# Graph network kernel: the second transposing pass of layer 1 written earlier, and layer 2's blocks written among layer 1's last blocks

## The chip, the cores and the metric

The kernel runs on one core of one Trainium2 chip. The metric is device time in microseconds (us). The kernel before took 1979.47 us, the median of 3 runs (1973.92 to 1994.36).

## What is computed

Four graph layers run over 2708 nodes with 128 features each. Every layer adds its result to `x` and normalises the row.

```python
x = _layernorm(x + _L0_gnn_ref(x, adj))   # msg = adj.T @ x, divided by the column sums of adj
x = _layernorm(x + _L1_gnn_ref(x, adj, ...))
x = _layernorm(x + _L2_gnn_ref(x, adj, ...))
x = _layernorm(x + _L3_gnn_ref(x, adj, ...))

# layer 1: messages over the edges, then an update of each row
messages = gelu(s[:, None, :] + d[None, :, :] + msg_b)      # s, d = x @ the two halves of msg_w
aggregated = einsum('ijd,ij->id', messages, adj)
h = gelu(concat(x, aggregated) @ upd_w.T + upd_b) + x       # then a layer norm

# layer 2: one dense product with adj, then a batch norm over the nodes
h = adj @ (x @ W) + b
h = gamma * (h - mean(h, 0)) * rsqrt(var(h, 0) + EPS) + beta
```

`adj` is 2708 x 2708 in float32 and has about 16 entries other than zero in a row. Layer 3 is an attention over the same edges.

## The kernel before

**Stages.** The rows of `adj` are cut into 22 blocks, 21 of 128 rows and one of 20 (`BLOCKS`). Layer 0 loads them one by one into a ring of nine buffers (`load`, L392 to L396, pool `ring`), multiplies each on TensorE (L411), and searches the entries of each row with VectorE (`extract`, L420 to L475). The 13 blocks of the first group (`SPLIT` = 13) are searched in layer 0. The other nine still stand in the ring when layer 1 starts, and are searched there. Each row's list of neighbours goes into a table in DRAM, sorted by the number of neighbours inside the two groups; `perm` holds which node stands at which place.

**Layer 1** goes over 22 blocks of sorted nodes. `own_row(b)` (L791) gathers the block's own rows. `messages(b)` (L797 to L827) gathers one neighbour at a time for all 128 rows with an indirect DMA on POOL's queue (`gather`, L236, issued at L237), `CAPS[b]` of them: 32, 24, 21, ... for the first group, and 31, 22, 20, 18, 17, 16, 14, 13, 10 for blocks 13 to 21. They are handled in chunks of up to eight, each chunk in one of five buffers `msg`. TensorE turns the own rows (L802) and multiplies them (L804), VectorE adds that product to the chunk (L813), ScalarE takes the Gelu (L816), and VectorE sums the neighbours up with their weights (L822, L824). The PSUM tile `own` has one buffer, so one block's messages are worked on at a time. `update(b)` (L829 to L865) multiplies the sums, normalises twice, writes the new rows `x_n` (L311) to DRAM by an indirect DMA of POOL's queue (`scatter`, issued at L245), turns `x_n` on TensorE (L860) and multiplies it by layer 2's weight (L864) into `xw[b]` (L865).

**The transposed matrix.** Layer 2 needs, for each block of sorted nodes, the matching columns of `adj`. `transposed(e, rows)` (L867 to L889) turns block `e` on TensorE (L877, 22 transposes), copies them on ScalarE (`at_sb`, three buffers, L882), and writes them to `at_dram` with seven DMAs of SP's queue (L884). The nine blocks of the second group are turned while they stand in the ring. The 13 of the first group are loaded a second time. In the program that is written after the updates of blocks 9 to 12, four, four, four and one at a time.

**Layer 2** is a loop of its own that is written behind layer 1. For each block `b` it gathers 128 rows of `at_dram` (L926, issued at L237; 1.39 MB), and adds 22 products into six PSUM banks `accs2` (L929; each float32 matmul is two instructions, so 44 for a block). A row of `at_dram` is whole only when all 22 blocks have been turned, so no block of layer 2 can be gathered before that. Behind it lie the batch norm (L985 to L1062) and layer 3.

**What sets the order.** Only VectorE in layer 0, and three engines in layer 3, follow the order of the program (`manual_schedule`). In layers 1 and 2 a planner lays out each engine's queue from the whole program; each queue is then worked through strictly in turn. The planner moves instructions a long way. In the kernel before, TensorE's queue holds all 484 transposes ahead of block 0 of layer 2, and that block stands ahead of the update of block 9, though the program writes layer 2 behind all of layer 1.

Below, A(e) stands for layer 2's block `e` (its gather, or its 44 TensorE instructions), and x2(b) for the writing of `x_n` of block `b`.

Of the kernel before, what the change touches and what calls it, by code (L numbers as in the profile page):

```python
# [9 lines left out]
FP = mybir.dt.float32  # L10
# [5 lines left out]
P = 128  # L16
N = 2708
D = 128
NFULL = N // P
NREM = N - NFULL * P  # L20
NBLK = NFULL + 1
# [19 lines left out]
SPLIT = 13  # L41
# [19 lines left out]
BLOCKS = [(b * P, min(P, N - b * P)) for b in range(NBLK)]  # L61


ORDER = [*range(20), 21, 20]
# [15 lines left out]
def gnn_resnorm_kernel(  # L80
# [21 lines left out]
    nc = tc.nc  # L102
# [103 lines left out]
    at_dram = tables.tile([NBLK * P, N], FP, name="at_dram")  # L206
# [7 lines left out]
    perm = keep.tile([P, NBLK], I32, name="perm")  # L214
# [21 lines left out]
    def gather(dst, table, index):  # L236
        nc.gpsimd.indirect_dma_start(  # L237
            out=dst,
            out_offset=None,
            in_=table[0:N, :],  # L240
            in_offset=bass.IndirectOffsetOnAxis(ap=index, axis=0),
        )
# [82 lines left out]
    def banks(name):  # L325
        return [bank.tile([P, 512], FP, name=f"{name}{i}", tag="bank") for i in range(6)]

    with ExitStack() as layer:
        ring = layer.enter_context(tc.tile_pool(name="ring", bufs=RING))
# [62 lines left out]
        def load(b):  # L392
            r0, n = BLOCKS[b]
            rows = ring.tile([P, N], FP, name="rows", tag="rows")
            nc.sync.dma_start(rows[0:n, :], adj[r0 : r0 + n, :])
            return rows  # L396
# [110 lines left out]
        def ranked(g):  # L507
            b0, b1 = GROUPS[g]
            rows = min(N, b1 * P) - b0 * P
            nc.vector.tensor_scalar(  # L510
                rank[:, b0:b1], above[g], 0.5, 0.5 * (rows - 1) + b0 * P, ALU.mult, ALU.add
            )
# [43 lines left out]
        def sorted_lists(g):  # L556
            b0, b1 = GROUPS[g]
            full = min(b1, NFULL)
            parts = [(b0, full, P)] + ([(NFULL, NBLK, NREM)] if b1 > full else [])
            for c0, c1, n in parts:  # L560
                nc.sync.dma_start(
                    ls[0:n, c0:c1, :],
                    lists_dram[c0 * P : c0 * P + (c1 - c0 - 1) * P + n, :].rearrange(
                        "(b p) w -> p b w", p=n
                    ),
                )
                nc.vector.tensor_copy(idx[0:n, c0:c1, :], ls[0:n, c0:c1, SLOTS : 2 * SLOTS])
                nc.vector.tensor_copy(perm[0:n, c0:c1], ls[0:n, c0:c1, 2 * SLOTS + 1])
                nc.vector.tensor_tensor(
                    wrong[0:n, c0:c1, 3], ls[0:n, c0:c1, 2 * SLOTS], caps[0:n, c0:c1], ALU.is_gt  # L570
                )

        def load3(b):

            k, j = BLOCKS3[b]
            mine_3 = lists3[:, b % 6, :]
            for r in range(4):
                r0 = BASE3[b] + r * j * k
                nc.sync.dma_start(
                    mine_3[32 * r : 32 * r + j * k, :], lists_dram[r0 : r0 + j * k, :]  # L580
                )
            n, r0 = 4 * j * k, BASE3[b]
            nc.sync.dma_start(
                node3[0:n, b, :], lists_dram[r0 : r0 + n, 2 * SLOTS : LW]
            )

        def beside3(b):

            if b < SPLIT + 2:
                return list(range(FIRST3))[2 * max(b - 3, 0) : 2 * max(b - 2, 0)]  # L590
            return list(range(FIRST3, NB3))[2 * (b - SPLIT - 2) : 2 * (b - SPLIT - 1)]
# [66 lines left out]
        def run(steps):  # L658
            for _ in steps:
                pass  # L660
# [31 lines left out]
        for jb in (20, 21):  # L692
            m, at = BLOCKS[jb][1], (jb - 20) * (D + 1) + D
# [95 lines left out]
        xw = xs  # L789

        def own_row(b):  # L791
            n = BLOCKS[b][1]
            x_s = mine.tile([P, D], FP, name="x_s", bufs=3)
            gather(x_s[0:n, :], x1_dram, perm[0:n, b : b + 1])
            return x_s

        def messages(b, x_s, three):  # L797
            n, kk = BLOCKS[b][1], CAPS[b]
            po = own_ps.tile([P, 512], FP, name="own", tag="own")
            x_st, s_ps = mine.tile([P, P], FP, name="x_st"), po[:, P : 2 * P]  # L800
            acc = (po[:, 0:P], po[:, 3 * P : 4 * P])
            nc.tensor.transpose(po[:, 0:n], x_s[0:n, :], ident[0:n, 0:n])  # L802
            nc.scalar.copy(x_st[:, 0:n], po[:, 0:n])
            nc.tensor.matmul(s_ps[0:n], lhsT=x_st[:, 0:n], rhs=ws_t, start=True, stop=True)  # L804
            parts = mine.tile([P, 2, D], FP, name="parts")
            cuts = chunks_of(kk)
            for c0, c1 in cuts:
                kc = c1 - c0
                msg = msgs.tile([P, 8, D], FP, name="msg")
                for k in range(kc):  # L810
                    gather(msg[0:n, k, :], d_dram, idx[0:n, b, c0 + k : c0 + k + 1])
                mk = msg[0:n, 0:kc, :]
                nc.vector.tensor_tensor(  # L813
                    mk, mk, s_ps[0:n].unsqueeze(1).to_broadcast((n, kc, D)), ALU.add
                )
                nc.scalar.activation(mk, mk, AF.Gelu)  # L816
                for k in range(c0, c1):
                    last, m = acc[k % 2][0:n], msg[0:n, k - c0, :]
                    to = parts[0:n, k % 2, :] if k >= kk - 2 else last
                    v = ls[0:n, b, k : k + 1]  # L820
                    if k < 2:
                        nc.vector.tensor_scalar(to, m, v, None, ALU.mult)  # L822
                    else:
                        nc.vector.scalar_tensor_tensor(to, m, v, last, ALU.mult, ALU.add)  # L824
            for i, b3 in enumerate(three):
                spread(b3, po, 256 + 64 * i)
            return x_st, parts  # L827
# [39 lines left out]
        def transposed(b, rows):  # L867

            r0, n = BLOCKS[b]
            for j0 in range(0, NBLK, 4):  # L870
# [9 lines left out]
                for a, e, m in ((0, full, P), (full, count, NREM)):  # L880
                    if e > a:
# [6 lines left out]
                            at[0:m, a:e, 0:n],  # L888
                        )  # L889

        ahead = own_row(0)
        waiting = None
        left = list(range(SPLIT, NBLK))
        for b in range(NBLK):
            if b == SPLIT - 2:
                sorted_lists(1)
            x_s, ahead = ahead, own_row(b + 1) if b + 1 < NBLK else None
            three = beside3(b)
            if b == 2 or b == SPLIT + 1:
                for b3 in beside3(b + 1):  # L900
                    load3(b3)
            for b3 in beside3(b + 2) if three or beside3(b + 1) else []:
                load3(b3)
            x_st, agg = messages(b, x_s, three)
            for _ in range(2 if b < 1 else 1):
                if left:
                    e = left.pop(0)
                    run(extract(e, rows_of[e]))
                    transposed(e, rows_of[e])
                    if e == SPLIT:  # L910
                        ranked(1)
                    if e == NBLK - 3:
                        run(place(SPLIT, NBLK - 2, lists(SPLIT, NBLK - 2)))
                    if e == NBLK - 1:
                        run(place(NBLK - 2, NBLK, lists(NBLK - 2, NBLK)))
            update(b, x_s, x_st, agg)
            if not left and b >= 9:
                for e in range(4 * (b - 9), min(SPLIT, 4 * (b - 8))):
                    transposed(e, load(e))


        accs2 = banks("acc2_")
        for b in range(NBLK):
            n = BLOCKS[b][1]
            at = ring.tile([P, N], FP, name="at_rows", tag="rows")
            gather(at[0:n, :], at_dram, perm[0:n, b : b + 1])  # L926
            for ib in range(NBLK) if b == 0 else ORDER:
                i0, m = BLOCKS[ib]
                nc.tensor.matmul(  # L929
                    accs2[ib // 4][0:m, (ib % 4) * D : (ib % 4 + 1) * D],  # L930
                    lhsT=at[0:n, i0 : i0 + m],
                    rhs=xw[0:n, b, :],
                    start=(b == 0 and ib % 4 == 0),
                    stop=(b == NBLK - 1 and ib in (3, 7, 11, 15, 19, 20)),
                )

# [19 lines left out]
    with ExitStack() as layer:  # L958
# [28 lines left out]
        for b0, count, n in quads():  # L987
            a = accs2[b0 // 4].rearrange("p (j d) -> p j d", d=D)[0:n, b0 % 4 : b0 % 4 + count]
            nc.vector.tensor_tensor(hb[0:n, b0 : b0 + count], a, broad(b_row, n, count), ALU.add)
            for b in range(b0, b0 + count):  # L990
                nc.tensor.matmul(
                    ps_m[:, 0:D], lhsT=ones[0:n, :], rhs=hb[0:n, b, :],
                    start=(b == 0), stop=(b == NBLK - 1),
# [4 lines left out]
        for b0, count, n in quads():  # L998
# [4 lines left out]
            for j in range(count):  # L1003
                nc.tensor.matmul(
                    ps_v[:, 0:D], lhsT=ones[0:n, :], rhs=sq[0:n, j, :],
                    start=(b0 + j == 0), stop=(b0 + j == NBLK - 1),
# [6 lines left out]
        for b0, count, n in quads():  # L1013
# [34 lines left out]
            for j in range(count):  # L1048
                at = slice(j * P, j * P + n)
# [17 lines left out]
    with ExitStack() as layer:  # L1067
# [341 lines left out]
        for i, (b, j) in enumerate(quads):  # L1409
            g, jj = BLOCKS3[b]  # L1410
            e = g * (P // g)
# [550 lines left out]
```

## Time and profile before

| what | value |
|---|---|
| median of 3 runs | 1979.47 us |
| the profiled execution, its own time | 1674.75 us |
| its span | 1673.0 us |
| layer 0 | up to about 224 us |
| first gather of layer 1 | 223.9 us |
| first gather of block 13's messages | 587.6 us |
| first and last gather of `at_rows` | 548.4 and 856.7 us |
| last TensorE instruction of L929 | 881.0 us, running |
| batch norm | 881 to 960 us |
| layer 3 | 960 to 1673 us |

The profiled execution is 304.7 us shorter than the median of the runs. No view shows why; sums below are made against the profiled execution.

The profile's groups give, for one line and one engine, busy time and the mean duration of one instruction, and behind the second bar the idle time just before and what ended most of it. The waits add up who waited for whom. The timeline gives the instructions of one engine in order of time: start, duration, line, and in brackets the idle time before. Windows give busy time by engine for a stretch. PE is TensorE, PEld its weight loads, DVE VectorE, ACT ScalarE, POOL GpSimd, and SPq the queue of SP.

### The profile page before, as it was taken

The numbers are of one execution on the slowest core, as the hardware profiler recorded it, in microseconds if no ns is written. First come the engines' busy times: TensorE is split into PE (matmuls) and PEld (weight loads), VectorE is DVE, ScalarE is ACT, GpSimd is POOL, SyncE is SP. The second block draws the span as 40 slices with busy tenths as digits, with TensorE's granted clock in tenths as the row PEclk, the third lists the DMA queues.
The fourth block names the chain that finished last, engine by engine and source line by source line (L and its number), as shares of the span: only waits on it lengthen the run. The fifth ranks groups of instructions, "written<-read, shape, count | busy, mean of one in ns | idle before, by whom it ended". The sixth has DMA issues, their size and how long they took to land. (4 is left out here: it accounts for less than half of the span.)

```text
span 1673.0 us, 24020 instructions
## 1 busy us (share of the span) xinstructions
PE 1197.2 (72%) x5876; PEld 850.9 (51%) x5876; DVE 1215.7 (73%) x5697; ACT 695.7 (42%) x2635; POOL 916.7 (55%) x1007
## 2 busy tenths in 40 slices
PE   5996654455626544463795769988989988998994
PEld 5996543334414533463684325554555555555553
DVE  9999966777747571455444479788889888898883
ACT  4959543433314120111111534454545545554552
POOL 0000247777775677777610578665656666666530
PEclk9997555555555666686796856776677777767675
DMA  9433277798937524342531687976666766867630
GB/s 352 179 128 123 50 213 170 206 230 239 258 90 181 168 60 117 119 148 84 190 138 45 201 273 206 233 215 190 192 191 203 214 190 166 231 190 221 190 92 8
DMA packets 162245, 288.49 MB, mean 172 GB/s; under 512 B 44342, under 2 KB 115890, under 8 KB 155015
## 3 DMA queue, kind: packets, MB, share of 16 engines
q0 software_dynamic: 61120, 191.23, 40.8%
q1 hardware_dynamic: 95893, 90.69, 17.5%
q10 hardware_dynamic: 5082, 4.94, 1.0%
q8 instruction: 49, 0.80, 0.2%
q14 instruction: 101, 0.83, 0.2%
HBM read 242.74 MB, written 43.97 MB: 171 GB/s over the span
## 5 line engine op out<-in xcount | busy, mean ns | idle before, releaser
L237 POOL DMA_INDIRECT g<-t_dram,idx x400 | 402.3, 1006 | 195.1 <-issue 133.4
L237 POOL DMA_INDIRECT msg<-d_dram,idx x398 | 376.9, 947 | 124.6 <-issue 103.6
L1254 ACT ACTIVATE sum_junk<-g 126x128 bf16<-126x128 f32 (+3 forms) x800 | 235.3, 296 | 117.0 <-DVE g L1246 66.1
L929 PE MATMUL acc<-x_nat,at_rows 128*128 128x128 f32 (+2 forms) x968 | 155.5, 318 | 119.9 <-DMA at_rows<-at_dram,perm 119.9
L1223 PE MATMUL z<-x,copies 32*126 32x512 f32 (+3 forms) x800 | 212.3, 887 | 30.4 <-DVE g L1423 29.7
L877 PE MATMUL pt_a<-ident,rows 128*128 128x128 f32 (+1 forms) x484 | 115.6, 393 | 145.8 <-ACT at_sb L882 145.6
L929 PEld LDWEIGHTS acc<-x_nat,at_rows 128*128 128x128 f32 (+2 forms) x968 | 140.0, 225 | 130.7 <-DMA at_rows<-at_dram,perm 110.8
L1423 DVE TENSOR_TENSOR g<-g,z 126x1536 f32<-126x1536 f32 (+3 forms) x100 | 174.9, 1749 | 11.5 <-PE z L1223 11.3
L877 PEld LDWEIGHTS pt_a<-ident,rows 128*128 128x128 f32 (+1 forms) x484 | 82.3, 202 | 173.1 <-ACT at_sb L882 172.0
L411 PE MATMUL acc<-x_nat,rows 128*128 128x129 f32 (+5 forms) x1188 | 155.1, 290 | 18.5 <-DMA rows<-in_adj_dram 18.5
L1228 PE MATMUL z<-g,ident 126*126 126x512 f32 (+3 forms) x200 | 166.2, 926 | 0.0
L411 PEld LDWEIGHTS acc<-x_nat,rows 128*128 128x128 f32 (+2 forms) x1188 | 148.8, 207 | 24.5 <-DMA rows<-in_adj_dram 19.3
L1254 ACT ACTIVATION_READ_ACCUMULATOR sum_junk<-g 126x1 f32 (+3 forms) x800 | 149.6, 187 | 0.0
L1300 PEld LDWEIGHTS po_s<-wm,g 126*128 126x128 f32 (+3 forms) x800 | 119.4, 233 | 43.3 <-DVE wm L1287 32.1
L1300 PE MATMUL po_s<-wm,g 126*128 126x24 f32 (+6 forms) x800 | 121.3, 306 | 25.2 <-DVE wm L1287 23.4
L824 DVE SCALAR_TENSOR_TENSOR own<-msg,ls,own 128x128 f32<-128x128 f32 (+1 forms) x310 | 108.1, 349 | 37.9 <-ACT msg L816 36.5
L813 DVE TENSOR_TENSOR msg<-msg,own 128x1024 f32<-128x1024 f32 (+4 forms) x58 | 61.8, 1065 | 95.3 <-PE own L804 63.6
L245 POOL DMA_INDIRECT lists_dram<-lists,rank x22 | 21.5, 978 | 183.0 <-DVE cv L435 162.5
L1246 DVE SCALAR_TENSOR_TENSOR g<-g,a_ps 126x1024 f32<-126x1024 f32 (+3 forms) x100 | 121.2, 1212 | 0.2 <-issue 0.2
L882 ACT COPY at_sb<-pt_a 128x512 f32<-128x512 f32 (+3 forms) x154 | 69.5, 479 | 116.4 <-DMA at_dram<-at_sb 112.3
L430 DVE FIND_INDEX8 ci<-cv,rows 128x8 uint32<-128x170 f32 (+1 forms) x352 | 114.7, 326 | 0.0
L435 DVE MAX8 cv<-rows 128x8 f32<-128x170 f32 (+1 forms) x352 | 110.8, 318 | 0.0
(283 smaller groups left out, 2135.6 us busy)
## 6 DMA issues: line engine op xcount, KB each, us to landing
rows<-in_adj_dram SPq DMA_DIRECT2D x34, 1354.0 KB
at_dram<-at_sb SPq DMA_DIRECT2D x105, 256.0 KB
g<-t_dram,idx POOLq DMA_INDIRECT x400, 4.6
msg<-d_dram,idx POOLq DMA_INDIRECT x398, 3.0
t_dram<-t_row SPq DMA_DIRECT2D x21, 256.0 KB
at_dram<-at_sb SPq DMA_DIRECT2D x21, 64.0 KB
x_dram<-x_nat SPq DMA_DIRECT2D x5, 256.0 KB
d_dram<-d_sb SPq DMA_DIRECT2D x5, 256.0 KB
```

The source lines that it names most:

```text
L237: nc.gpsimd.indirect_dma_start(out=dst, out_offset=None, in_=table[0:N, :], in_offset=bass.IndirectOffsetOnAxis(ap=index, axis=0),)
L411: nc.tensor.matmul(accs0[k][0:m, c0 : c0 + f1 - f0], lhsT=rows[0:n, j0 : j0 + m], rhs=x_nat[0:n, b, f0:f1], start=k not in started, stop=( ...
L430: nc.vector.max_index(out=ci[0:n, at], in_max=cv[0:n, at], in_values=rows[0:n, c0 : c0 + cw])
L435: nc.vector.max(out=cv[0:n, 8 * s : 8 * s + 8], in_=rows[0:n, c0 : c0 + cw])
L877: nc.tensor.transpose(pt[0:m, j, 0:n], rows[0:n, c0 : c0 + m], ident[0:n, 0:n])
L929: nc.tensor.matmul(accs2[ib // 4][0:m, (ib % 4) * D : (ib % 4 + 1) * D], lhsT=at[0:n, i0 : i0 + m], rhs=xw[0:n, b, :], start=(b == 0 and i ...
L1223: nc.tensor.matmul(z3[0:e, r, :] if r < 3 else z1[0:e], lhsT=copies[g][rows, j, :], rhs=own[b][1][rows, :], start=True, stop=r < 3, skip_g ...
L1228: nc.tensor.matmul(z1[0:e], lhsT=ident[0:e, 0:e], rhs=g4[0:e, 3, 0:HD], start=False, stop=True, skip_group_check=True,)
L1246: nc.vector.scalar_tensor_tensor(z, z, 0.0, a_ps[0:e].unsqueeze(1).to_broadcast((e, 2, HD)), ALU.max, ALU.mult)
L1254: nc.scalar.activation(junk[0:e], g4[0:e, r, hd * D : (hd + 1) * D], AF.Identity, accum_out=sc[0:e, r, hd : hd + 1],)
L1300: nc.tensor.matmul(po[:, p0 * HEADS : (p0 + g) * HEADS], lhsT=g4s[i][0:e, r, HD : HD + D], rhs=wm[0:e, 4 * i + r, :, :], start=True, stop= ...
L1423: nc.vector.tensor_tensor(z, z, z3[0:e], ALU.add)
```

## The change

Layer 2's block becomes a function `layer2(b)`. The second loads and transposes of the first group are written one after each update from block 1 on, two after blocks 9 and 10. The six banks are taken after the update of block 11, and from there on two blocks of layer 2 are written after each update, blocks 0 and 1 after block 11 up to block 20 after block 21. Block 21 of layer 2 follows.

```diff
+        accs2 = []
+
+        def layer2(b):
+            n = BLOCKS[b][1]
+            at = ring.tile([P, N], FP, name="at_rows", tag="rows")
+            gather(at[0:n, :], at_dram, perm[0:n, b : b + 1])
+            for ib in range(NBLK) if b == 0 else ORDER:
+                i0, m = BLOCKS[ib]
+                nc.tensor.matmul(
+                    accs2[ib // 4][0:m, (ib % 4) * D : (ib % 4 + 1) * D],
+                    lhsT=at[0:n, i0 : i0 + m],
+                    rhs=xw[0:n, b, :],
+                    start=(b == 0 and ib % 4 == 0),
+                    stop=(b == NBLK - 1 and ib in (3, 7, 11, 15, 19, 20)),
+                )
+
+        again = list(range(SPLIT))
         ahead = own_row(0)
-        waiting = None
         left = list(range(SPLIT, NBLK))
...
             update(b, x_s, x_st, agg)
-            if not left and b >= 9:
-                for e in range(4 * (b - 9), min(SPLIT, 4 * (b - 8))):
+            for _ in range(2 if b in (9, 10, 11) else 1):
+                if b and again:
+                    e = again.pop(0)
                     transposed(e, load(e))
-
-        accs2 = banks("acc2_")
-        for b in range(NBLK):
...
+            if b == 11:
+                accs2.extend(banks("acc2_"))
+            if b >= 11:
+                for e in range(2 * (b - 11), min(b, 2 * (b - 10))):
+                    layer2(e)
+        layer2(NBLK - 1)
```

More of the change, by code (lines that the diff above doesn't have):

```diff
@@ L916, in gnn_resnorm_kernel @@
             update(b, x_s, x_st, agg)
-            if not left and b >= 9:
-                for e in range(4 * (b - 9), min(SPLIT, 4 * (b - 8))):
+            for _ in range(2 if b in (9, 10, 11) else 1):
+                if b and again:
+                    e = again.pop(0)
                     transposed(e, load(e))
-        accs2 = banks("acc2_")
-        for b in range(NBLK):
[L924 to L935, printed above, removed]
+            if b == 11:
[4 more added lines that the diff above has]
+        layer2(NBLK - 1)
         nc.vector.tensor_tensor(wrong[:, :, 1], wrong[:, :, 1], cnt, ALU.subtract)
```

## The prediction, made before the changed kernel was run

> **What bounds the kernel now.** I read the windows first, cut at the start of layer 1, at block 13 of layer 1, at the last messages, at the end of layer 2 and at layer 3:
>
> ```profile
> 224.00:588.00 364.00, 184.67 (x844) 145.92 (x843) 242.55 (x1298) 129.58 (x301) 261.13 (x275) 0.58 0.74 197
> 588.00:831.00 243.00, 122.03 (x680) 108.76 (x679) 115.40 (x476) 41.06 (x103) 181.51 (x192) 0.67 0.39 112
> 831.00:881.00 50.00, 49.68 (x375) 44.19 (x375) 23.00 (x109) 8.28 (x27) 7.31 (x11) 0.94 0.41 163
> ```
>
> The columns are PE, PEld, DVE, ACT, POOL, the granted clock, DMA share, GB/s. POOL is busy 181.5 of 243 us in the middle stretch, and more it can't be, as its gathers show:
>
> ```profile
> L237 POOL DMA_INDIRECT msg<-d_dram,idx x398 | 376.9, 947 | 124.6 <-issue 103.6
> ```
>
> A gather takes 0.95 us and 0.30 us pass before the next, 1.25 in all; 192 instructions x 1.25 = 240 us of 243. So layer 1 lasts as long as POOL's queue from 224 to about 830. From 831 to 881 POOL is idle and PE is full. The waits from 588 to 882 say what happened to PE before:
>
> ```profile
> PE acc L929 <- DMA at_rows<-at_dram,perm: 102.1, 10, 28.1
> DVE msg L813 <- PE own L804: 51.9, 8, 27.4
> POOL x_dram L245 <- DVE x_n L311: 29.2, 3, 11.6
> ```
>
> PE stood 102 us before a block of layer 2 whose gather was still far back in POOL's queue. The last row is POOL waiting for x2(19), x2(20), x2(21), the end of its work. PE's timeline has the two speeds of a layer 2 block, and the backlog:
>
> ```profile
> 644.04 7.62 PE L929 MATMUL acc<-x_nat,at_rows 128*128 128x128 f32 x44 [28.13 <-DMA at_rows<-at_dram,perm]
> ...
> 847.22 8.80 PE L929 MATMUL acc<-x_nat,at_rows 128*128 128x128 f32 x72
> ...
> 867.75 13.70 PE L929 MATMUL acc<-x_nat,at_rows 128*128 128x128 f32 x94
> ```
>
> 44 instructions take 7.6 us after a wait and 8.80 x 44/72 = 5.4 running on. Of 968, 342 lie behind 830.7, nearly 8 blocks, 50 us with the updates between them. That backlog is what the change can remove.
>
> **The second transposes.** In the changed program they come much earlier, but the planner had brought them forward before. In the built queues, up to the turning of x_n of blocks 0 to 6, PE has done 153, 212, 254, 287, 324, 371, 426 transposes before and 135, 184, 236, 276, 320, 374, 430 after; all 484 stand ahead of A(0) in both, at the same place. The work is the same: 13 loads, 286 transposes, 91 writes. One stall matters here, in SP's queue:
>
> ```profile
> SPq L579 <- DMA lists_dram<-lists,rank: 23.4, 1, 23.4
> ```
>
> SP reads lists that POOL has not yet scattered; 33 of the 154 writes of `at_dram` stand behind it before, 32 after. Behind it POOL idles 5.6 + 2.8 + 2.8 = 11 us at 515 to 528. The lists' scatters keep their places in POOL's queue, so I cost this part at nothing. It hides behind POOL, which has 1.25 us of work on every gather until then. If SP came through early, up to 11 us, and 4 us of gathers waiting for gathers at 271 to 277, would come back; if loads moved forward crowd the DMA engines (0.95 busy at 350 to 400) it costs as much. I take 0.
>
> **Layer 2 in pairs.** POOL still issues 398 + 22 + 22 + 22 gathers and scatters. What moves: before the last message gather stand 20 blocks of layer 2 instead of 15, so that gather comes 5 x 1.25 = 6 us later; and the `at_rows` come two at a time behind a block's messages. PE takes both ahead of the turning of x_n, so the next block's own product, and with it all of its messages on VectorE, waits for two gathers and two products instead of mostly one. A queue moved past has a price too: the scatters x2(b). Before, x2(17) stands in the middle of block 20's gathers and x2(18) in block 21's. After, x2(17) stands ahead of all of block 19's, x2(18) of block 20's, x2(19) of block 21's. While a scatter waits for x_n, every later gather waits.
>
> I follow the chain from block 13's first gather (587.6 us, called 0), with four measured steps: a gather lands 6.4 us after its issue (637.6 to 644.04), its pair 2 later (1.39 MB at the 425 GB/s of 832 to 839 is 3.3 us, less the 1.25 between issues); a block costs 8 then 5.5 us or 7.6 us each; from the end of the products to the next own product about 5.5 us (744.08 to 749.96); from there to x_n of the block before 10.5 us (725.5 to 736.4, 749.96 to 760.1, 810.5 to 820.3). POOL's place times 1.25 gives the issue.
>
> Block 13: A(4) is issued at 30, lands at 36.4, and PE has one of its products ahead of block 13's own product, 37. Before that was at 19, but A(5) then held block 14 until 78 (665.9); after, block 14's own product is at 62. Block 15: A(6), A(7) issued 74 and 76, products end about 94, own product 100 (before 114). Block 16: A(8), A(9) issued 105 and 106, own product 132 (before 138). Block 17: 158 (162). Block 18: 183 (195). Block 19: 211 (223). Block 20: 234 (243). Here the order turns: A(18) is issued at 234 with the stalls below, lands at 241, A(18) and half of A(19) stand ahead of update 20, the rest ahead of block 21's own product, about 260 (before 255). Then messages 7 us, update 21 to x_n 11 us, xw at 281, A(21) cold 7 us: end at 287 or 288.
>
> On the way x2 must be ready at its place. From a block's last gather to its x2 the queue leaves 35, 27, 26, 22 us for blocks 16 to 19. By the chain x_n(16) is ready at 169 where POOL comes at 167, x_n(18) at 217 where it comes at 212; the others are in time. Stalls 2 + 5 = 7 us, contained above. Before, the end is 881.0 - 587.6 = 293.4. Gain 293.4 - 287 = 6 us, between +13 (no stall) and -5 (each step 1 us longer). The stages behind keep their work and start earlier by it.
>
> **A rule against it.** [...] The change breaks up the one long run of layer 2 (clock 0.94 in 831 to 881) into pairs that follow waits. [...] by the row it is 7.6 against 5.4, 18 us more. I take the row[...]. And it falls into the 102 us that PE waits anyway; only A(18), A(19) and A(21) lie on the chain, where I have it in.
>
> **The rivals.** *The short lead decides (slower).* In the profile x_n follows its block's last gather by 47.5, 43.6, 50.0, 54.8, 56.2 us for blocks 15 to 19. If that stays and the queue leaves 44, 35, 27, 26, 22, POOL stalls 3 and 9 us, and then for each what it lacks less the stall just before: 12, 17, 17. Sum 58 us; less the gain, about +50. The change is slower than before from 13 us of stalls on. Against: in the profile this lag is PE's wait for single `at_rows` in the middle of updates; undisturbed blocks 0 to 4 have 38 to 42, with the row searches beside them, and the chain gives 28 to 38.
>
> *The first half gains too (faster).* The loads spread evenly (DMA 0.78 at 250 to 350, 0.95 after) and SP comes earlier to its stall: 11 + 4 us, and without the 7 us of stalls the second half gives 13: 28 us. If the 304.7 us by which the runs are longer stretch all alike (1979.5/1673 = 1.18), 33 us. For it: PE's 102 us of waits are the largest in the stretch. Against: SP's stall is set by POOL's scatters.
>
> *Nothing moves.* The planner had interleaved before, so the same work in the same queues ends within 3 us: 1979.
>
> **How the numbers follow.** Gains of the profiled execution are carried to the median as they are, stretched at most by 1.18. The likeliest: 6 x 1.18, about 7 us, 1979.5 - 7.5 = 1972, its own range 1962 to 1985, chance 0.5 (0.05 of it beyond 1%). Faster rival 1979.5 - 33 = 1946, chance 0.3. Nothing moves, 1979, 0.1. Short lead, 1979.5 + 50 = 2030, 0.1, left out of the range but for its mild end. One per cent is 20 us, about what a measurement of this kernel can tell from no change: faster 0.3 + 0.05 = 0.35, same 0.45 + 0.1 = 0.55, slower 0.1. Range 1942 to 1990.
>
> **What would show it.** In the profile after: the first half ends within 5 us of 588; `at_rows` gathers come in pairs; PE's waits for them stay near 100 us in total but the run without gaps at the end shrinks from 50 us to under 20; block 21's own product comes about 27 us before the end of layer 2 (38 before the change); POOL waits for x_n ahead of blocks 18 and 20 by some us. I am wrong if POOL waits for x_n by more than 13 us in total before block 21's last gather (slower), or if block 13's first gather comes 10 us sooner (faster).

## The result, and the profile after

The changed kernel takes 1986.68 us, the median of 20 runs (1971.9 to 2000.27); the kernel before takes 1987.26 us in 20 runs beside them (1973.92 to 2002.62). The ratio is 1.0004, with a 95% interval of 0.9983 to 1.0026. So there is no change that can be measured; the forecast had been 1972 us, 0.4% less. Here and below, runs more than 1.5% above the fastest of their kernel are left out of the ratios; this concerns only the run with six buffers (3 of 20) and the runs of the kernel before on that chip (4 of 57).

The execution of 1674.75 us that the prediction's sums are made against stands alone: every other execution of the kernel before took 1972 us or more. The profiled execution after the change took 1996.29 us (span 1994.4 us), like the others. So the kernel before was profiled again (the first experiment, span 1996.2 us), and below "before" is that second profile unless the 1673 us span is named.

The windows by stage, after the change: layer 1 up to block 13's first gather, from there to the last message gather, to the end of layer 2, the batch norm, and layer 3. The columns are those of the prediction.

```profile
224.00:687.40 463.40, 189.84 (x845) 149.88 (x844) 246.12 (x1295) 127.78 (x301) 261.81 (x275) 0.57 0.55 155
687.40:1025.00 337.60, 168.83 (x843) 141.25 (x842) 123.02 (x506) 41.66 (x105) 183.89 (x194) 0.63 0.32 100
1025.00:1077.00 52.00, 36.50 (x211) 31.25 (x211) 19.79 (x83) 8.07 (x24) 5.32 (x9) 0.70 0.10 33
1077.00:1166.90 89.90, 52.98 (x200) 36.03 (x199) 38.28 (x155) 31.29 (x89) 22.40 (x25) 0.73 0.37 114
1166.90:1994.40 827.50, 665.49 (x2516) 380.12 (x2516) 585.63 (x2424) 334.71 (x1936) 429.66 (x434) 0.66 0.57 162
```

The same stages in the second profile of the kernel before:

```profile
224.00:691.10 467.10, 188.95 (x801) 148.80 (x802) 242.02 (x1276) 124.67 (x296) 258.88 (x272) 0.55 0.54 152
691.10:1002.00 310.90, 125.20 (x653) 110.05 (x653) 115.57 (x470) 39.54 (x97) 177.85 (x189) 0.62 0.28 86
1002.00:1069.00 67.00, 60.46 (x414) 52.94 (x414) 24.41 (x118) 9.85 (x32) 11.06 (x15) 0.83 0.34 131
1069.00:1157.70 88.70, 51.02 (x200) 34.22 (x200) 38.22 (x155) 31.27 (x89) 22.42 (x24) 0.75 0.37 116
1157.70:1996.20 838.50, 660.72 (x2516) 376.09 (x2516) 584.74 (x2424) 334.63 (x1936) 427.82 (x434) 0.66 0.56 160
```

Two things are to be seen. The change did what it says: behind the last message gather stand 211 TensorE matmuls instead of 414, and this tail is 52 us instead of 67. But the messages take 338 us from block 13 on instead of 311. So 15 us are gained in the tail and 27 are paid for it ahead of it; the first stage is 4 us shorter. Layer 2 ends at 1076.8 instead of 1069.0 us. Layer 3 has the same work in both and differs by 11 us, so single executions scatter by as much. POOL, busy 181.5 of 243 us of the middle stage in the 1673 us span, is busy 178 of 311 before and 184 of 338 after. Counted as in the prediction, with the 0.30 us between two gathers, that is 240 of 243 there, and 236 of 311 and 242 of 338 here. Its gathers last as long as they did, but it stands idle 176.5 us ahead of them (175.1 before) where the 1673 us span had 124.6:

```profile
L237 POOL DMA_INDIRECT msg<-d_dram,idx x398 | 377.8, 949 | 176.5 <-issue 138.0
```

What TensorE waited for in the middle stage shows what changed there. Waits after the change, between 687 and 1025 us:

```profile
PE acc L900 <- issue: 70.2, 65, 2.5
POOL x_s L237 <- issue: 46.2, 6, 12.5
...
ACT agg_t L840 <- PE acc L900: 20.2, 1, 20.2
ACT x_nt L862 <- PE acc L900: 19.2, 1, 19.2
...
PE acc L900 <- DMA at_rows<-at_dram,perm: 10.3, 1, 10.3
```

And before, between 691 and 1002 us:

```profile
PE acc L929 <- DMA at_rows<-at_dram,perm: 55.9, 6, 14.8
...
PE acc L929 <- issue: 18.8, 11, 3.1
```

The wait for the gathered rows shrank from 55.9 to 10.3 us, and in its place stands "issue", 18.8 us before and 70.2 after, in 65 pieces of at most 2.5 us: TensorE stands between two products of the same block, and nothing in the profile holds it. Behind it ScalarE waits for the end of the products, up to 20 us at a time. TensorE's timeline shows a pair of layer-2 blocks, A(6) and A(7), after the change:

```profile
788.53 10.39 PE L900 MATMUL acc<-x_nat,at_rows 128*128 128x128 f32 x71 [10.33 <-DMA at_rows<-at_dram,perm]
799.75 0.27 PE L900 MATMUL acc<-x_nat,at_rows 128*128 128x128 f32 x1 [0.83 <-issue]
801.17 0.41 PE L900 MATMUL acc<-x_nat,at_rows 128*128 128x128 f32 x2 [1.15 <-issue]
803.30 0.37 PE L900 MATMUL acc<-x_nat,at_rows 128*128 128x128 f32 x1 [1.73 <-issue]
...
817.33 0.37 PE L900 MATMUL acc<-x_nat,at_rows 128*128 128x128 f32 x1 [2.43 <-issue]
...
825.03 0.60 PE L900 MATMUL acc<-x_nat,at_rows 128*128 128x128 f32 x2 [0.30 <-issue]
```

The first 71 of the pair's 88 instructions take 10.4 us. The other 17 take 27 us: most last 0.37 us, and ahead of most lie 0.8 to 2.4 us of nothing. The pair costs 37 us, 16 of products and 21 of gaps. The next two have 76 and 59 such instructions at the start and cost 31 and 37 us. In the kernel before, a single block after a wait can fit into the start:

```profile
800.79 6.94 PE L929 MATMUL acc<-x_nat,at_rows 128*128 128x128 f32 x44 [6.46 <-DMA at_rows<-at_dram,perm]
```

It has such stretches too, but fewer. A(12) and A(13) come together at 973 to 1009 and take 36 us, with parts of an update between them. A(4) stands alone and still runs out after 38 instructions:

```profile
759.67 6.04 PE L929 MATMUL acc<-x_nat,at_rows 128*128 128x128 f32 x38 [13.20 <-DMA at_rows<-at_dram,perm]
...
773.28 0.37 PE L929 MATMUL acc<-x_nat,at_rows 128*20 128x128 f32 x1 [3.13 <-issue]
```

The stretches go with POOL's gathers. After the change POOL's gathers ahead of three of its waits end at 821.1, 860.8 and 899.0 us, and TensorE's gaps end at 825.0, 863.1 and 901.2. In the tail, when POOL no longer gathers messages, the products come with hardly a gap in both kernels: after the change 66 of them take 10.04 us from 1033.66 on, and between 1025 and 1077 us none waits at "issue"; before, TensorE is busy 60.5 of the tail's 67 us. In the 1673 us span all of this group's idle time, 119.9 us, is put down to the gathered rows and none to "issue", though POOL gathers there as well. The start that runs without a gap holds 71, 76 and 59 instructions in three pairs after the change and 38 at A(4) before; what ends it, no run shows.

### The profile page after: what moved, and what is told of

Read it like the earlier page. It is cut to its first block, busy times and chain, and to the rows that moved or that the text cites. A ratio compares the mean times of both kernels' runs of the same rounds, so it can differ in the third digit from the quotient of the medians.

```text
span 1994.4 us, 24011 instructions
## 1 busy us (share of the span) xinstructions
PE 1287.6 (65%) x5876; PEld 902.3 (45%) x5876; DVE 1226.1 (61%) x5697; ACT 696.0 (35%) x2635; POOL 919.6 (46%) x1007
## 5 line engine op out<-in xcount | busy, mean ns | idle before, releaser
L237 POOL DMA_INDIRECT msg<-d_dram,idx x398 | 377.8, 949 | 176.5 <-issue 138.0
L1232 PE MATMUL z<-x,copies 32*126 32x512 f32 (+3 forms) x800 | 222.8, 939 | 58.8 <-issue 33.6
L900 PE MATMUL acc<-x_nat,at_rows 128*128 128x128 f32 (+2 forms) x968 | 174.9, 334 | 93.2 <-issue 70.2
L900 PEld LDWEIGHTS acc<-x_nat,at_rows 128*128 128x128 f32 (+2 forms) x968 | 153.4, 238 | 109.3 <-issue 92.2
L1237 PE MATMUL z<-g,ident 126*126 126x512 f32 (+3 forms) x200 | 175.1, 972 | 0.0
L1309 PE MATMUL po_s<-wm,g 126*128 126x24 f32 (+6 forms) x800 | 137.7, 330 | 39.7 <-DVE wm L1296 35.3
L1309 PEld LDWEIGHTS po_s<-wm,g 126*128 126x128 f32 (+3 forms) x800 | 135.5, 260 | 58.4 <-DVE wm L1296 41.3
L1232 PEld LDWEIGHTS z<-x,copies 32*126 32x126 f32 (+3 forms) x800 | 64.0, 257 | 100.0 <-issue 65.9
L1247 DVE SCALAR_TENSOR_TENSOR g<-z,a 126x128 f32<-126x128 f32 (+3 forms) x400 | 91.9, 286 | 24.9 <-issue 12.0
```

The lines of the kernel that those rows point to most:

```text
L237: nc.gpsimd.indirect_dma_start(out=dst, out_offset=None, in_=table[0:N, :], in_offset=bass.IndirectOffsetOnAxis(ap=index, axis=0),)
L900: nc.tensor.matmul(accs2[ib // 4][0:m, (ib % 4) * D : (ib % 4 + 1) * D], lhsT=at[0:n, i0 : i0 + m], rhs=xw[0:n, b, :], start=(b == 0 and i ...
L1232: nc.tensor.matmul(z3[0:e, r, :] if r < 3 else z1[0:e], lhsT=copies[g][rows, j, :], rhs=own[b][1][rows, :], start=True, stop=r < 3, skip_g ...
L1237: nc.tensor.matmul(z1[0:e], lhsT=ident[0:e, 0:e], rhs=g4[0:e, 3, 0:HD], start=False, stop=True, skip_group_check=True,)
L1309: nc.tensor.matmul(po[:, p0 * HEADS : (p0 + g) * HEADS], lhsT=g4s[i][0:e, r, HD : HD + D], rhs=wm[0:e, 4 * i + r, :, :], start=True, stop= ...
```

## Experiments

Three theories stood against each other. **S (supply):** while POOL gathers, TensorE gets instructions more slowly than it can run them, so the number of instructions in the messages' path costs time, and not their work alone. **L (short lead):** the scatters x2, earlier in POOL's queue, stop it until x_n is ready (24 us in the trace after, at blocks 16, 17, 18 and 19). **B (buffer):** POOL is stopped at the gather of own rows, which have three buffers. Every ratio is to the kernel before on the same chip; chips differ (its median was 1987 to 1991 us in four sets of runs and 2020 in one).

**The kernel before, unchanged,** for a profile.

> The kernel before, unchanged, for a second profile. The profile of it that the sums were made against took 1674.75 us, the 20 runs of it 1974 to 2003. If the 300 us belong to that one execution, this one takes 1975 to 2000 us, and its stages last about as long as in the profile after the change: layer 1 and 2 from 224 to about 1040, layer 3 about 830 us. POOL then has idle stretches between gathers in layer 1 as in the profile after. If instead the change made layer 1 slower and something else paid for it, layer 1 and 2 end here well before 1040 and layer 3 is longer than 830.

Measured: 1998.01 us. Layer 1 and 2 end at 1069 us and layer 3 lasts 838 us, POOL's gathers have idle stretches of 8 to 14 us before own rows. So the missing 300 us belong to that one execution, and the sums of the prediction were made against an execution that no other run resembles.

**Part one alone.**

```diff
+        again = list(range(SPLIT))
...
-            if not left and b >= 9:
-                for e in range(4 * (b - 9), min(SPLIT, 4 * (b - 8))):
+            for _ in range(2 if b in (9, 10, 11) else 1):
+                if b and again:
+                    e = again.pop(0)
                     transposed(e, load(e))
```

> Only the first part of the change: the second loads and transposes written from block 1 on; layer 2 stays a loop behind layer 1. Theory A (the planner had already placed both, nothing moves): ratio to before within 0.3% of 1. Theory B (a gain of one part is paid back by the other): this part alone is off by 0.5% or more, faster (10 to 30 us) if the loads were crowded before.

Measured: 0.9989 (0.9966 to 1.0013). Nothing measurable, as step two of the prediction had it; layer 2 ends at 1064.4 us.

**Part two alone,** from block 12 on; blocks 20 and 21 of layer 2 come at the end.

```diff
+            if b == 12:
+                accs2.extend(banks("acc2_"))
+            if b >= 12:
+                for e in range(2 * (b - 12), 2 * (b - 11)):
+                    layer2(e)
+        layer2(NBLK - 2)
         layer2(NBLK - 1)
```

> Only the second part, one block later than in the change so that all transposes are written ahead of it: layer 2 two by two from block 12's update on, blocks 20 and 21 at the end; the second transposes stay behind updates 9 to 12. Theory A (nothing moves): ratio within 0.3% of 1. Theory B (the parts cancel): 0.5% or more from 1, with the sign opposite to that of the first part alone. The prediction's chain gave this part 6 us, 0.3%.

Measured: 1.0061 (1.0039 to 1.0082), 12 us slower; layer 2 ends at 1074.4 us. So the pairs are no gain alone but a loss. That the early transposes pay for it is not shown: alone they are within the noise.

**The kernel before with layer 2's products cut** to 2 of 22 for blocks 1 to 20; the others are left out.

```diff
-            for ib in range(NBLK) if b == 0 else ORDER:
+            for ib in range(NBLK) if b == 0 else ORDER if b == NBLK - 1 else (0, 4):
```

> The kernel before with 2 of the 22 products left out... of the 22 products only 2 are made for blocks 1 to 20 of layer 2: 800 of its 968 TensorE instructions are left out, all gathers stay. It bounds what any placing of layer 2's products can bring. If a backlog of TensorE at the end of layer 2 decides, as in the profile of the 1674.75 us execution (50 us, nearly 8 blocks), it is 40 us or more faster, 0.98. If the products are hidden in the runs, it is within 10 us of before.

Measured: 0.9769 (0.9738 to 0.9799), 46 us faster. Layer 2 ends at 1019 instead of 1069 us, and the last message gather comes at 966 instead of 1002. Of the 50 us, 36 are won ahead of the tail: the products burden the messages more than the end. With the gathers where they are, no placing of the products can bring much more than this.

**One block of layer 2 after each update.**

```diff
-                for e in range(2 * (b - 11), min(b, 2 * (b - 10))):
-                    layer2(e)
-        layer2(NBLK - 1)
+                layer2(b - 11)
+        for e in range(11, NBLK):
+            layer2(e)
```

> The changed kernel, but one block of layer 2 behind each update from block 11 on, and blocks 11 to 21 behind layer 1. Theory S (supply: while POOL gathers, TensorE runs its first 60 to 76 instructions of a stretch without gaps and then gets one per 1 to 2.5 us, so that a pair of 88 costs 31 to 37 us and a single block of 44 about 7): faster than the changed kernel by 0.5 to 1%. Theory L (the early x2 scatters make POOL wait for x_n, 24 us): also faster, since fewer gathers stand in front; POOL's waits for x_n are then gone while single blocks of layer 2 still cost as much as in pairs. Theory N (placing makes no difference): within 0.3%.

Measured: 0.9981 (0.9957 to 1.0004). This run tells less than it was made for: the planner laid the queues as for a loop at the end (layer 2 ends at 1064.2 us, and its gathers from block 9 on are issued within 1 us of those of the run with part one alone). What is written one by one is not executed one by one.

**Six buffers for own rows.** `name="x_s", bufs=3` becomes `bufs=6`.

> The changed kernel with six buffers instead of three for a block's own rows. In its trace POOL stands still 83 us in all ahead of the own-row gathers of blocks 14 to 21, each released by the update two blocks back, which frees the third buffer. Theory B (this buffer holds POOL up, and POOL sets layer 1's end): 20 to 60 us faster, 0.97 to 0.99. Theory S (TensorE's supply sets the pace, POOL's waits follow from it): less than 10 us, 0.995 to 1.0; the waits move to the messages' buffers.

Measured: 0.995 (0.9925 to 0.9976), 10 us. The waits moved to the scatters x2:

```profile
POOL x_dram L245 <- DVE own L824: 56.5, 6, 19.3
...
POOL x_dram L245 <- DVE x_n L311: 17.7, 3, 7.0
```

Between 687 and 1017 us POOL waits 74 us there, where in the changed kernel it had waited 83 us for own rows and 24 for x_n. So B accounts for 10 us of the 83; the rest of the wait is only moved.

**The scatters x2 three blocks later.**

```diff
-            scatter(x2_dram, perm[0:n, b : b + 1], x_n[0:n, 0, :])
+            done.append((b, x_n))
...
+            if len(done) > 3:
+                written()
```

`x_n` also gets five buffers, and what is left over is written at the end.

> The changed kernel with the scatter x2 of a block written three blocks later. Theory L (short lead: POOL's 24 us of waits for x_n ahead of block 21's last gather are what eats the gain): the waits are gone and it is 15 to 25 us faster, 0.99. Theory S: POOL waits as long at the next gather that needs a freed buffer, and the time is within 0.4%.

Measured: 1.0095 (1.0065 to 1.0124), slower by 19 us. The waits for x_n are gone from the middle stage and POOL stands at the own rows instead:

```profile
POOL x_s L237 <- issue: 61.8, 6, 20.0
...
POOL x_s L237 <- PE own L804: 24.3, 2, 12.2
POOL x_s L237 <- DVE own L824: 12.4, 1, 12.4
```

So taking L's waits away brings nothing. That it costs 19 us, S had not expected either. In its trace A(16), with an update in between, takes 45 us, and for 23 us of that time no engine but POOL runs a single instruction (the columns are those of the windows above):

```profile
999.76:1023.12 23.36, 0.00 (x0) 0.00 (x0) 0.00 (x0) 0.00 (x0) 16.82 (x19) 0.59 0.50 175
```

ScalarE's next instruction (L840) needs TensorE's products of L833, which end at 999.3; it runs at 1027.4. No wait in the profile accounts for that, and why it fell here is open. As the stall is longer than the loss of 19 us, the run is no clean test of L.

**Few wide products in place of many.** The sums come out transposed, and are turned back.

```diff
-            for ib in range(NBLK) if b == 0 else ORDER:
...
-                nc.tensor.matmul(
-                    accs2[ib // 4][0:m, (ib % 4) * D : (ib % 4 + 1) * D],
-                    lhsT=at[0:n, i0 : i0 + m],
-                    rhs=xw[0:n, b, :],
...
+            for g in range(6):
+                i0, i1 = g * 512, min(N, g * 512 + 512)
+                nc.tensor.matmul(
+                    accs2[g][:, 0 : i1 - i0], lhsT=xw[0:n, b, :], rhs=at[0:n, i0:i1],
...
+        for g in range(6):
...
+            nc.vector.tensor_copy(turned[:, i0:i1], accs2[g][:, 0 : i1 - i0])
+        for ib in range(NBLK):
...
+            nc.tensor.transpose(
...
```

> The changed kernel with layer 2's product the other way round: xw as the weights and 512 columns of the gathered rows moving, 12 TensorE instructions for a block in place of 44 (264 in all for 968); the sums then stand transposed and are turned back at the end with 6 copies and 44 TensorE instructions. By the 0.89 us that a 512-column instruction takes elsewhere in the trace (L1188), a block is 10 us of TensorE work in place of 5.4, so by work alone it is 20 to 60 us slower. Theory S (the number of instructions counts, not their work): blocks cost about 10 us also in pairs, messages end 20 us or more sooner, and in all it is 10 to 40 us faster, 0.98 to 0.995.

Measured: 0.9896 (0.9817 to 0.9975). The group of layer 2's products says the rest:

```profile
L900 PE MATMUL acc<-at_rows,x_nat 128*128 128x512 f32 (+2 forms) x264 | 162.4, 754 | 79.9 <-DMA at_rows<-at_dram,perm 78.9 <-ACT x_nat L865 1.1
```

against, in the changed kernel,

```profile
L900 PE MATMUL acc<-x_nat,at_rows 128*128 128x128 f32 (+2 forms) x968 | 174.9, 334 | 93.2 <-issue 70.2 <-DMA at_rows<-at_dram,perm 22.1 <-ACT x_nat L865 0.3
```

TensorE is busy with these products for 162 us in 264 instructions instead of 175 in 968, so their work is about the same (the 10 us per block that the expectation feared did not come; 12 instructions take some 7). The 70 us of "issue" ahead of the products are gone, and the last message gather comes at 983 instead of 1025 us. This is what S expects, but the edit changes more than a count: the weight loads, too, fall from 968 with 153 us of busy time to 264 with 63. The runs do not part the two.

**Wide products in the kernel before's order.** The same edit of layer 2 in its loop.

> The kernel before (layer 2 as a loop behind layer 1, second transposes behind updates 9 to 12), with the 12 wide instructions per block of layer 2 and the turning back at the end. Theory S: here too fewer instructions keep TensorE supplied while POOL gathers: 0.985 to 0.995 of the kernel before. If only the pairs' places suffered from the supply, it is no faster than the kernel before, 0.997 to 1.01, as the wide products are more work in the tail behind the last messages.

Measured: 0.9883 (0.9846 to 0.9919). The gain is not one of the pairs: the kernel before gains as much. Yet its products had only 28 us of "issue" ahead of them in all, against 70 in the changed kernel, so this idle time does not measure what the wide products win.

**Wide products and six own-row buffers.**

> The changed kernel with wide products and six own-row buffers. If the two effects add (1.0 - 0.9896 and 1.0 - 0.995), 0.985. If they free the same wait, 0.990.

Measured: 0.9955 (0.9933 to 0.9976), neither expectation. The buffers, which gave 0.5% with the narrow products, take some of the gain of the wide ones: the same kernel with three buffers had 0.9896, with an interval that overlaps this one, and 0.9867 (0.9832 to 0.9902) in the run further down. All three are on different chips. Which wait does it was not tried.

**The changed kernel with the products cut,** the edit of the cut above: 20 of 22 products are left out for blocks 1 to 20.

> The changed kernel with only 2 of the 22 products made for blocks 1 to 20 of layer 2; all gathers stay in their new places. The same cut in the kernel before gave 0.977. Theory S (the cost of the pairs is TensorE's products): no difference to that, 0.973 to 0.981. If the places of the gathers and of the scatters x2 in POOL's queue cost time by themselves, it is 10 us or more slower than that cut, 0.982 or above.

Measured: 0.9697 (0.965 to 0.9743). Without the products the pairs are not slower than the loop, if anything faster (0.9769 there, on another chip). In the profiles layer 2 ends at 1024.6 with pairs, on a chip that takes 1.5% longer, and at 1019.1 without, so the order of these two is not settled.

**Wide products, pairs against loop on one chip.** The second of these has part one of the change and layer 2 as a loop behind layer 1.

> The changed kernel with wide products once more, beside the next one on the same chip. If the pairs' place gains by itself (0.7% between the two cuts to 2 of 22 products) and the supply of instructions took it back, this is 0.4% or more faster than the same kernel with layer 2 as a loop behind layer 1. If the place brings nothing, the two agree within 0.3%.

> Wide products, the second transposes written early as in the change, layer 2 as a loop behind layer 1. Ratio to the kernel before 0.985 to 0.99, as the wide products gave with the transposes in the old place (0.9883); against the pairs see there.

Measured: pairs 0.9867 (0.9832 to 0.9902), loop 0.9822 (0.9793 to 0.9852), 1962.07 and 1952.16 us. The pairs bring nothing by themselves; the loop is ahead by 10 us at the medians, with intervals that overlap a little. Of the versions that leave no products out, the loop with wide products and early transposes is the fastest found, 1.8% faster than the kernel before.

Side by side, from the profiles, one execution each (us):

| | last message gather | end of layer 2 |
|---|---|---|
| before, second profile | 1002.0 | 1069.0 |
| part one alone (loop) | 997.0 | 1064.4 |
| changed (pairs) | 1025.0 | 1076.8 |
| part two alone (pairs) | 1039.2 | 1074.4 |
| wide, early, loop | 974.3 | 1028.0 |
| wide, early, pairs | 986.0 | 1039.3 |

For the wide products the end is that of the products, ahead of the turning back. In each of these comparisons of like with like the pairs end layer 2 some 5 to 12 us later. Each is a difference of two single executions, and these scatter by as much; the medians point the same way, 12 us for part two alone and 10 for the wide products.

## Why the prediction was wrong

**The second transposes at nothing: right.** 0.9989, and the first half ends at 687 instead of 691 us, within the 5 us allowed (the 588 belonged to the other execution).

**Pairs leave a shorter tail: right.** The gathers come in pairs (858.6 and 859.9, 896.8 and 898.1), the matmuls behind the last message gather fall from 414 to 211, no run without gaps at the end is longer than 16 us (under 20 was foretold), and block 21's own product stands 28 us ahead of the end instead of 38 (27 was foretold). TensorE's waits for the rows, which were to stay near 100 us, fell to 10.

**What a pair costs: wrong, and this is the failing step.** The prediction took "a block costs 8 then 5.5 us or 7.6 us each" from the timeline of the 1673 us span. After the change six pairs in a row, A(6) to A(17), take 37, 31, 37, 32, 32 and 37 us in place of 13.5, in four of them with parts of an update in between. Their products alone take 14 to 18 us; gaps ahead of the products, nearly all at "issue", add 3 to 21. In the 1673 us span the products had no such gaps. The chain of own products, counted from block 13's first gather, shows where it decides:

| block | 14 | 15 | 16 | 17 | 18 | 19 | 20 | 21 | end |
|---|---|---|---|---|---|---|---|---|---|
| before | 102 | 150 | 184 | 229 | 266 | 296 | 328 | 340 | 378 |
| after | 90 | 144 | 185 | 225 | 259 | 295 | 345 | 361 | 389 |
| after less before | -12 | -6 | 0 | -4 | -8 | 0 | +18 | +21 | +12 |
| predicted difference | -16 | -14 | -6 | -4 | -12 | -12 | -9 | +5 | -6 |

Up to block 18 no sign contradicts the prediction. That is luck rather than support for the sums: from block 14 to 21 the kernel before is itself 24 to 85 us later than in the 1673 us span, and the two delays nearly cancel. They no longer do at block 20. From block 19's own product to block 20's the chain had 23 us and the changed kernel takes 50; the kernel before takes 32 where its 1673 us span had 20. A(16) and A(17) fill 37 of the 50 us, from 983.4 to 1020.6, where 13.5 were set down: 17 us of products, 12 of gaps at "issue", 8 of an update, in which TensorE waits 4.8 for x_n. The next step was mis-sized too. From the end of the products to the own product 12 us pass instead of 5.5, as ScalarE starts to copy the own row only 9.7 us after TensorE turned it, with no releaser recorded:

```profile
1022.29 0.37 PE L802 MATMUL own<-ident,x_s 128*128 128x128 f32 x1 [1.73 <-issue]
...
1032.33 0.27 ACT L803 COPY x_st<-own 128x128 f32<-128x128 f32 x1 [27.78 <-remote]
```

In the kernel before, the same copy follows within 0.5 us (1018.00 after 1017.54). So the pair is the largest term that was too small, and this step is the second. The way from block 19 to block 20 costs 27 us more than foretold, while the kernel before loses 12 there itself, and the difference goes from 0 to +18 where it was to go from -12 to -9.

**POOL as the bound: wrong.** "A gather takes 0.95 us and 0.30 us pass before the next" still holds, but that fills only 236 of 311 us. POOL is stopped ahead of the own-row gathers until an update frees one of the three buffers. After the change own row 18 is issued at 873.0, 1.3 us after update 15's Gelu at 871.6, and own row 19 at 913.4, after update 16's at 912.1. The updates come late: for blocks 13 to 20 x_n follows its block's last gather by 65 to 81 us in the second profile before, where the 1673 us span had 44 to 57. After the change it is 62 to 66 for blocks 13 to 16 and 43 to 54 for the other four. With six buffers only 10 of 83 us came back.

**POOL's waits for x_n: mis-sized, and not shown to cost time.** Set at 7 us, measured 24 ahead of block 21's last gather, beyond the 13 named as the sign of a loss: 4.3, 7.3, 10.4 and 1.9 us ahead of the scatters at 923.65, 949.43, 991.17 and 1011.62, and each time the gather behind it starts 0.3 us after the scatter's end. But with late scatters they are gone and nothing is gained. So the short-lead rival had its symptom right; that the waits cost time of their own, no run shows.

**The clock: priced wrongly.** The prediction took the row of 7.6 us as the price of a block after a wait, but that row holds two speeds. In it, 644.04 to 651.66, the granted clock is 0.50 up to 648.57 and 1.00 from there. The first 4.53 us hold 21 instructions, 0.22 us each, and the other 3.09 us show 25, two of them begun earlier, 0.12 us each. After the change A(20) and A(21) show the same two rates: 0.21 and 0.22 us at 0.50, 0.12 and 0.11 at 1.00. So between these two clocks an instruction's time differs by a factor of 1.7 to 1.9, and 7.6 us is a block of which a part ran at 1.00 already. A pair all at 0.50 would take 88 x 0.216 = 19 us of products in place of 13.5 (an estimate from these rates); 14 to 18 were measured. So the clock explains at most some 4 of the up to 24 us by which a pair is dearer; the gaps and what lies between the products are the larger part.

**From the profiled execution to the median: wrong.** "Gains of the profiled execution are carried to the median as they are" supposed that the missing 305 us were spread over the same limits. They were not: most of the time stands as idle time at "issue" and "remote", in layer 3 too (838 us for 713). A profile 15% shorter than every run should have been asked which of its limits the runs share. The rival "nothing moves" had the number, 1979 for 1987 us, but not the reason: the tail moved by 15 us and the messages gave it back. That the sum is nothing is luck.

What is open: where the gaps at "issue" come from that stand in TensorE's products while POOL gathers, and why the pairs still end layer 2 some 11 us later with wide products, where no "issue" is left ahead of the products.

## What to carry to other kernels

When work is moved from a long run at the end into the gaps of an earlier stage, price it by the same instructions in that stage under load, and by how many come in a row, not by their rate in the long run: here a single block after a wait took 6.9 us, and six pairs 31 to 37 us each where 13.5 had been set down. If "issue" grows where a wait for data shrinks, count instructions before moving them again: wider ones, here 12 for 44, gained 1.0 to 1.8% (0.5% with six own-row buffers) where no placing gained anything. And before summing against one profiled execution, check that its time is that of the runs.

## What the runs showed of the hardware

The gaps are not TensorE's alone, as the copy of ScalarE and the 23 us above show. In the second profile of the kernel before, VectorE searches the rows while POOL gathers the first messages:

```profile
249.06 0.09 DVE L430 MATCH_VALUE_LOAD ci<-cv,rows 128x8 f32 x1 [3.56 <-issue]
...
253.25 0.09 DVE L430 MATCH_VALUE_LOAD ci<-cv,rows 128x8 f32 x1 [3.55 <-remote]
...
256.76 0.09 DVE L430 MATCH_VALUE_LOAD ci<-cv,rows 128x8 f32 x1 [2.87 <-remote]
```

In the 1673 us span the same instructions follow each other without a gap:

```profile
244.72 0.07 DVE L430 MATCH_VALUE_LOAD ci<-cv,rows 128x8 f32 x1
...
245.26 0.07 DVE L430 MATCH_VALUE_LOAD ci<-cv,rows 128x8 f32 x1
...
245.80 0.07 DVE L430 MATCH_VALUE_LOAD ci<-cv,rows 128x8 f32 x1
```

In both profiles that the text compares, the delayed instructions keep to a common beat. The starts 249.06, 253.25 and 256.76 above lie 6 and 5 times 0.70 us apart, and TensorE's from 803.30 to 825.03 after the change are all multiples of it apart, to within 0.05 us. VectorE's delayed starts at 804.74 and 805.45 fall on TensorE's 804.73 and 805.45. So the delays of the two engines do not look independent; what they share, no run shows. The two DMA queues that the pages call "instruction" do not stand out: the 1673 us span and the profile after the change both list 49 and 101 packets, 0.80 and 0.83 MB, with 0.2% or less of the DMA time each.

Up to 224 us, before the first gather of messages, the 1673 us span and that after the change agree to within 1 us of busy time on every engine. And the page of the 1673 us execution gives a landing time for the message gathers ("x398, 3.0"); the page after the change lists the 398 without one. The trace of the first holds some 28,500 semaphore events, that after the change 13,500. One rival to S follows from this and stands untested: that the recording of events holds the engines back, and that fewer instructions help because there is less to record. Every run here was recorded, so none can tell. Whether the missing records and the gaps have one cause stays open.
